# Four gate columns of a graph network's GRU: from a Strassen product for two gates and a plain product for two, to one Strassen product of seven 384-column blocks that shares PSUM banks

## The chip, the cores and the metric

The kernel runs on one core of one Trainium2 chip. The metric is the time of one execution in device microseconds (us), as the median of several runs. Beside the timed runs there is one execution under the hardware profiler; every row, share and moment quoted here comes from that one.

## What is computed

64 graphs of 256 nodes with 256 channels go through two layers. Cut to what matters here, the reference says:

```python
# layer 0
x = layernorm(x + (D^-1/2 adj D^-1/2 + alpha I) @ x @ W.T + b)
# layer 1, x_in has 512 channels
x_conv = relu(bn2(conv17(relu(bn1(conv1(x))))) + x)        # along the nodes
x_nmp  = exp(-dist(x)) @ relu(x @ w_msg.T + b_msg)
x_in   = concatenate([x_conv, x_nmp])
gi = x_in @ w_ih.T + b_ih                                  # 3 * 256 columns: r, z, n
gh = x    @ w_hh.T + b_hh                                  # 3 * 256 columns
r = sigmoid(gi_r + gh_r);  z = sigmoid(gi_z + gh_z)
x = layernorm(x + (1 - z) * tanh(gi_n + r * gh_n) + z * x)
```

Per graph the gates are thus a product of a 256 x 768 input (256 channels of x, 512 of x_in) with weights. Columns r and z need all 768 inputs and add up; column n has to keep its part from x (gh_n) apart from its part from x_in (gi_n), since r multiplies only the first. Counted that way there are four gate columns of 256: r, z, gh_n and gi_n.

## The kernel before, in words

Everything is float32. The 64 graphs go in four quarters (q) of 16 (Q). For each quarter, `layer0` and `layer1` run per graph and leave the spectrum of a 17-tap convolution; the convolution itself is done for the quarter at once, as products by frequency (`products`, matmuls at L542, with combinations of the results on VectorE (DVE) at L585 and L586) and an inverse transform made of many small DVE instructions (`real_transform`, `complex_begin`, `complex_end`). Its result goes to DRAM, and the gates (`gru(g)`) read it back graph by graph.

**What `gru(g)` does.** `load_gate(g + 1)` brings x1 of the next graph (`x_g`, L787) and its transposed inputs (`inputs`, 512 KB, L789) from DRAM through SyncE's (SP's) queue; both tiles have two buffers. `load_conv(g + 2)` (L777) brings the convolution's result for the graph after that. `transposed(g + 1)` makes the last two of the six 128-channel blocks of `inputs`: for graphs of the last quarter and the first four of every quarter (`in_blocks`) a DVE block transpose (L812), an addition on GpSimd (POOL, L813), a small one (L814) and two ScalarE (ACT) activations (L816); for all others TensorE (PE) transposes (L822) and two activations (L824). `input_sums(g + 1)` makes four sums S of quarters of the input on POOL (L833 to L838, 128 x 384 elements each).

The gates r and z are one Strassen-Winograd product. The input is cut into four quarters A11, A12, A21, A22 (two node halves c, two channel halves of three 128-channel blocks) and the weights likewise; four weight quarters are replaced by differences T1 to T4. `block(p, j, a, b)` is one block product: three matmuls of 128 x 128 by 128 x 256 (L854) into half a bank. Seven of them go into the half banks of `p15`, `p26`, `p7` and `p34`, and DVE and ACT combine them in `trz` (L867 to L878). gh_n and gi_n are then a plain product for each node half c: two and four matmuls of 256 columns (L891) into the two halves of a bank `p_n`. DVE and ACT finish from L896 on: bias, r times gh_n, tanh (L903), the mix with z and x1 (L914 to L916), the layernorm (DVE statistics L326 to L328, an inverse root by `pow` on POOL at L329, L332, then two activations at L334), and a store of x1 to `out` from ACT's queue (L918). `trz` and `nn` have one buffer each; PSUM has four rotating banks for these products and for the convolution's (`accbank`), and four more for everything else.

**What sets the order of the work.** Each engine has its own in-order queue, filled by a scheduler from the order of the Python generators. `gru` yields four times; drivers interleave its pieces with other generators. By that, a graph's gates stand in one of four surroundings: between the layers of later graphs (`early` and `others`); between the convolution's products (`take(late, ...)` in the loop over `STEPS`); nearly by themselves with the inverse transform's DVE work inserted behind marked instructions (`paced`, `mark`, `RATES`); or quite by themselves, for the last quarter (`run(gates(q, range(Q)))`).

Of the kernel before, what the change touches and what calls it, by code (L numbers as in the profile page):

```python
# [26 lines left out]
def kernel(  # L27
# [128 lines left out]
    wrz = const.tile([P, 7, HALF, D], F32)  # L156
    B11, B21, B22, T1, T2, T3, T4 = range(7)
    wn = const.tile([P, 3 * DCH, D], F32)
# [265 lines left out]
    def x1_transposed(g):  # L424
# [7 lines left out]
        nc.scalar.copy(xn[:, 1], p[:, 1])  # L432

    def layer1(g, place):
# [4 lines left out]
        x1T = xn[:, :DCH]  # L439
# [80 lines left out]
        nc.scalar.copy(xn[:, DCH:], p)  # L520
# [115 lines left out]
    def turned(re, im, angle):  # L636


        t = freq.tile([P, 2, D], F32, name="turn", bufs=3)
        x, y = M[:, re, :], M[:, im, :]  # L640
        real_part(t[:, int(re > im), :], x, y, angle)
        return imaginary_part(t[:, int(re < im), :], x, y, angle), t
# [4 lines left out]
    def real_transform():  # L647
# [17 lines left out]
        for i, x, y in ((1, 9, 13), (2, 10, 14), (3, 15, 11)):  # L665
            angle = math.pi * ORDER[i] / 8
            t = freq.tile([P, 2, D], F32, name="turn", bufs=3)
# [50 lines left out]
    def output(q, n, re, im):  # L718
# [4 lines left out]
        t = freq.tile([P, 2, D], F32, name="turn", bufs=3)  # L723
# [61 lines left out]
    def load_gate(g):  # L785
# [5 lines left out]
        if in_blocks(g):  # L791
            FIRST[g] = gate.tile([1, N], F32, name="x1_first")
# [14 lines left out]
    def transposed(g):  # L807
# [3 lines left out]
        if in_blocks(g):  # L811
            behind(nc.vector.transpose(xcT.rearrange("p k (s r) -> p k s r", r=RB), CONV.pop(g)))  # L812
            nc.gpsimd.tensor_tensor(xcT, xcT, inputs[:, :DCH], op=ALU.add)  # L813
# [16 lines left out]
    def input_sums(g):  # L830
        A11, A12, A21, A22 = halves(GATE[g][1])
        S = SUMS[g] = gate.tile([P, 4, HALF, P], F32, name="sums", bufs=1)
        nc.gpsimd.tensor_tensor(S[:, 0], A21, A22, op=ALU.add)  # L833
        second = nc.gpsimd.tensor_tensor(S[:, 1], S[:, 0], A11, op=ALU.subtract)  # L834

        with tc.issue_after(second.ins):
            nc.gpsimd.tensor_tensor(S[:, 2], A11, A21, op=ALU.subtract)
            nc.gpsimd.tensor_tensor(S[:, 3], A12, S[:, 1], op=ALU.subtract)  # L838

    def gru(g):  # L840
# [5 lines left out]
        trz = gate.tile([P, 4, D], F32, name="trz", bufs=1)  # L846
        nn = gate.tile([P, NCH, D], F32, name="nn", bufs=1)
# [4 lines left out]
        def block(p, j, a, b):  # L852
            for k in range(HALF):
                nc.tensor.matmul(  # L854
                    p[:, j * D : (j + 1) * D], a[:, k], wrz[:, b, k], start=k == 0, stop=k == HALF - 1
                )

        p15, p26 = accbank("p_rz"), accbank("p_rz")
        block(p15, 0, A11, B11)
        block(p26, 0, A12, B21)  # L860
        block(p15, 1, S[:, 0], T1)
        block(p26, 1, S[:, 1], T2)
        yield
        if following:
            sent(g + 1)
        first = gate.tile([P, 2, D], F32, name="first", tag="gn")
        nc.scalar.copy(first, half(p15))  # L867
        mark(nc.vector.tensor_add(trz[:, 0:2], first[:, 0:1].to_broadcast([P, 2, D]), half(p26)), 1)
        p7, p34 = accbank("p_rz"), accbank("p_rz")
        block(p7, 0, S[:, 2], T3)  # L870
        block(p34, 0, S[:, 3], B22)
        block(p34, 1, A22, T4)
        nc.vector.tensor_add(trz[:, 3], trz[:, 1], p7[:, :D])
        mark(nc.vector.tensor_add(trz[:, 1:3], trz[:, 1:4:2], half(p34)), 1)

        nc.scalar.activation(trz[:, 0:4:2], trz[:, 0:4:2], AF.Tanh, scale=0.5)
        nc.vector.tensor_add(trz[:, 1:4:2], trz[:, 1:4:2], first[:, 1:2].to_broadcast([P, 2, D]))
        nc.scalar.activation(trz[:, 1:4:2], trz[:, 1:4:2], AF.Tanh, scale=0.5)  # L878
        if following:
            transposed(g + 1)  # L880
        yield
        for c in range(NCH):
            terms = [(inputs[:, k, c * P : (c + 1) * P], wn[:, k]) for k in range(3 * DCH)]
            if c == 0 and following:
                input_sums(g + 1)
            if c == 1 and g % Q + 2 < Q:
                load_conv(g + 2)
            p = accbank("p_n")
# [297 lines left out]
```

## Time and profile before

| | |
|---|---|
| timed runs | median 2135.34 us of 3 (2130.76 to 2136.28) |
| the profiled execution | 2128.84 us, span from first to last instruction 2127.1 us |
| TensorE clock granted, mean | 0.99 |
| instructions | 29,376 |
| DVE busy, whole span | 1430.8 us (67%) |
| ACT busy | 879.8 us (41%) |
| POOL busy | 691.1 us (32%) |
| HBM traffic | 296 MB, 139 GB/s over the span |

The profile has a page (busy time of each engine, a picture in 40 slices, the chain of work that ended last, the costliest groups of equal instructions) and a trace that can be asked for windows of time, a timeline and waits. "PE" is the matmul side of TensorE and "PEld" its loading of the stationary operand, which overlaps. A float32 matmul stands in the trace as two PE instructions, each with a PEld instruction of its own; so one block product of three matmuls is six rows. Since matmuls are pipelined, a matmul's own duration overlaps the next one's: its price is the distance from start to start. A row of a group reads: source line, engine, operation, output and inputs, shape, number of instructions | busy time in us, mean ns of one | idle time of the engine before them and what ended it. In the timeline a row is: start in us, duration, engine, line, operation, output and inputs, number of instructions, and in brackets how long the engine had idled and what released it.

### The profile page before, as it was taken

Reading aid. Unit: us, or ns where it says so; the run is one execution under the profiler, and the core shown is the slowest. Engines: PE = TensorE matmul, PEld = TensorE weight load, DVE = VectorE, ACT = ScalarE, POOL = GpSimd, SP = SyncE. Lnnn points to the kernel's source line nnn. Section 1 sums busy time; section 2 is a strip of 40 time slices with the busy share of each in tenths; the row PEclk is TensorE's granted clock in tenths of the full one; section 3 lists DMA queues with packets and bytes.
Section 4 is the critical chain, followed back from the end, with each engine's and each line's share of the span. In section 5 each row is a group of like instructions: output and inputs, shape, how many; then the busy total and the mean of one; then the engine's idle time right before and its main releaser. Section 6 shows DMA issues by size and latency. Waiting matters only on the chain. (4 is left out here: it accounts for less than half of the span.)

```text
span 2127.1 us, 29376 instructions
## 1 busy us (share of the span) xinstructions
PE 2036.4 (96%) x9693; PEld 1736.0 (82%) x9693; DVE 1430.8 (67%) x3467; ACT 879.8 (41%) x2113; POOL 691.1 (32%) x672
## 2 busy tenths in 40 slices
PE   6999999888999999999999999999999999999998
PEld 5888788766888888787888888877888888888887
DVE  5555567775558687774545978775454889976665
ACT  4666643456431234455553123445554122233332
POOL 3445310121431243213321224323331124455553
PEclk9999999999999999999999999999999999999999
DMA  4766656444447644333335754434333745443331
GB/s 125 236 200 196 199 188 210 148 134 123 106 132 219 193 126 133 100 117 101 115 99 157 225 156 132 119 102 132 94 94 99 244 148 141 117 119 95 95 90 50
DMA packets 302918, 298.26 MB, mean 140 GB/s; under 512 B 84112, under 2 KB 281572, under 8 KB 302766
## 3 DMA queue, kind: packets, MB, share of 16 engines
q1 hardware_dynamic: 242814, 200.37, 31.8%
q10 hardware_dynamic: 44480, 67.39, 8.9%
q0 software_dynamic: 15472, 28.61, 6.1%
q8 instruction: 78, 1.28, 0.2%
q14 instruction: 74, 0.61, 0.1%
HBM read 193.19 MB, written 103.06 MB: 139 GB/s over the span
## 5 line engine op out<-in xcount | busy, mean ns | idle before, releaser
L854 PE MATMUL p_rz<-wrz,sums 128*128 128x256 f32 x1536 | 350.9, 381 | 4.7 <-DVE gn L897 4.7
L891 PE MATMUL p_n<-wn,inputs 128*128 128x256 f32 x1536 | 349.2, 380 | 0.0
L854 PEld LDWEIGHTS p_rz<-wrz,sums 128*128 128x128 f32 x1536 | 289.8, 190 | 49.4 <-issue 10.9
L891 PEld LDWEIGHTS p_n<-wn,inputs 128*128 128x128 f32 x1536 | 287.0, 190 | 43.3 <-issue 6.6
L854 PE MATMUL p_rz<-wrz,inputs 128*128 128x256 f32 x1152 | 270.4, 379 | 0.0
L854 PEld LDWEIGHTS p_rz<-wrz,inputs 128*128 128x128 f32 x1152 | 217.9, 190 | 29.2
L370 POOL TENSOR_TENSOR dis<-deg,neg_half 128x2 f32<-128x2 f32 x64 | 46.5, 726 | 540.9 <-DVE deg L368 539.7
L329 POOL TENSOR_TENSOR ln_rs<-ln_rs,neg_half 128x2 f32<-128x2 f32 x129 | 98.8, 766 | 377.8 <-DVE ln_rs L328 349.3
L542 PE MATMUL p_k<-u,VM 128*128 128x256 f32 x736 | 175.1, 381 | 3.9 <-DMA u<-ud 3.0
L903 ACT ACTIVATE nn<-gn 128x256 f32<-128x256 f32 x128 | 53.4, 417 | 270.6 <-DVE gn L900 270.6
L833 POOL TENSOR_TENSOR sums<-inputs 128x384 f32<-128x384 f32 x64 | 66.0, 1031 | 292.2 <-ACT inputs L824 232.7
L542 PEld LDWEIGHTS p_k<-u,VM 128*128 128x128 f32 x736 | 139.0, 190 | 24.2 <-DMA u<-ud 3.2
L447 PE MATMUL p_conv<-wc,xn 128*128 128x259 f32 x512 | 131.6, 397 | 26.6 <-DVE xn L431 25.3
L400 PE MATMUL p_hT<-adjT,x 128*128 128x256 f32 x512 | 125.7, 387 | 15.8 <-DVE adjT L382 13.6
L447 PEld LDWEIGHTS p_conv<-wc,xn 128*128 128x128 f32 x512 | 97.2, 196 | 49.1 <-DVE xn L431 32.5
L509 DVE TENSOR_TENSOR aT<-aT,adjT 128x512 f32<-128x512 f32 x64 | 44.5, 696 | 122.0 <-ACT aT L508 122.0
L410 PE MATMUL p_out<-w,hT 128*128 128x256 f32 x512 | 123.1, 383 | 1.3 <-ACT hT L405 0.7
L483 PE MATMUL p_dft<-fwd,h 128*128 128x240 f32 x512 | 116.8, 371 | 6.4 <-ACT scols L451 6.4
L468 PE MATMUL p_msg<-wmsg,xn 128*128 128x256 f32 x512 | 121.3, 380 | 0.5 <-ACT inputs L824 0.5
L516 PE MATMUL p_nmp<-aT,msg 128*128 128x256 f32 x512 | 121.1, 379 | 0.2 <-DVE aT L509 0.2
L334 ACT ACTIVATE x_g<-x_g,ln_mr,ln_rs 128x256 f32<-128x256 f32 x128 | 70.0, 593 | 123.3 <-DVE ln_mr L332 123.3
L400 PEld LDWEIGHTS p_hT<-adjT,x 128*128 128x128 f32 x512 | 92.8, 192 | 31.8 <-ACT dist_l L498 6.2
(164 smaller groups left out, 3822.1 us busy)
## 6 DMA issues: line engine op xcount, KB each, us to landing
u<-ud SPq DMA_DIRECT2D x284, 256.0 KB
xn_d<-xn ACTq DMA_DIRECT2D x64, 512.0 KB
inputs<-xn_d SPq DMA_DIRECT2D x64, 512.0 KB
ud<-u_set POOLq DMA_DIRECT2D x39, 480.0 KB, 6.0
adj_t<-in_adj_dram SPq DMA_DIRECT2D x64, 256.0 KB
x_t<-in_x_dram SPq DMA_DIRECT2D x64, 256.0 KB
x_d<-x ACTq DMA_DIRECT2D x64, 256.0 KB
xc_d<-VM SPq DMA_DIRECT2D x64, 256.0 KB
```

The lines of the kernel that those rows point to most:

```text
L329: nc.gpsimd.tensor_tensor(rs[:, : len(chunks)], rs[:, : len(chunks)], neg_half[:, : len(chunks)], op=ALU.pow)
L334: nc.scalar.activation(y[:, c, :], y[:, c, :], AF.Identity, bias=mr[:, c : c + 1], scale=rs[:, c : c + 1])
L400: nc.tensor.matmul(p[:, k, :], x1[:, mc, k * P : (k + 1) * P], adjT[:, mc, 1 - mc : 3 - mc, :].rearrange("p n q -> p (n q)"), start=mc == ...
L410: nc.tensor.matmul(p[:, c, :], hT[:, k, c * P : (c + 1) * P], w0[:, k, :], start=k == 0, stop=k == DCH - 1)
L447: nc.tensor.matmul(p, x1T[:, k, c * P : (c + 1) * P], wc1[:, k, :], start=k == 0, stop=k == DCH - 1)
L468: nc.tensor.matmul(p[:, c, :], x1T[:, k, c * P : (c + 1) * P], wmsg[:, k, :], start=k == 0, stop=k == DCH - 1)
L483: nc.tensor.matmul(p[:, t0 * FL : t1 * FL], h[:, c, k * P : (k + 1) * P], fwd[:, first : first + t1 - t0, :].rearrange("p t f -> p (t f)") ...
L516: nc.tensor.matmul(p[:, k, :], msg[:, mc, k * P : (k + 1) * P], aT[:, mc].rearrange("p n q -> p (n q)"), start=mc == 0, stop=mc == NCH - 1,)
L542: nc.tensor.matmul(p[:, j * D : (j + 1) * D], v[:, k, :], u[:, k, :], start=k == 0, stop=k == DCH - 1)
L833: nc.gpsimd.tensor_tensor(S[:, 0], A21, A22, op=ALU.add)
L854: nc.tensor.matmul(p[:, j * D : (j + 1) * D], a[:, k], wrz[:, b, k], start=k == 0, stop=k == HALF - 1)
L891: nc.tensor.matmul(p[:, o * D : (o + 1) * D], lhsT, w, start=j == 0, stop=j == len(part) - 1)
```

## The change

The four gate columns become one Strassen-Winograd product. Each weight quarter now holds, for half of the 256 outputs (HD = 128), three groups of 128 columns for each 128-channel block: [gh_n, r, z] for a block of x, [r, z, gi_n] for a block of x_in. A bank holds the four groups in the order gh_n, r, z, gi_n, so the block of x writes columns 0 to 383 and the two blocks of x_in columns 128 to 511. For this the blocks of `inputs` are put in another order (x, x_nmp, x_nmp, x, then x_conv), so that each channel half begins with one block of x. Seven block products of three matmuls with 384 columns replace seven block products with 256 columns and the twelve plain matmuls.

Three of the seven products are not given a bank of their own: they are added onto a bank that ACT or DVE has read before, with one other product in between. The results are put together in one tile `G` (one buffer), by quarters (c, h): node half c and output half h. Nonlinear work is done on both node halves at once at the end.

The pieces of `gru` are now two, each of two sub-pieces: it yields SOFT inside a piece and HARD at its end, and in the loop over `STEPS` a new driver, `take_whole`, takes whole pieces (where a step took 0, 1 or 2 of the old four). The other changes follow from these: `sums` becomes four tiles with one buffer each, filled in the order 0, 1, 2 and later 3; `x1_first` has one buffer instead of two, `turn` two instead of three; the weights are loaded and prepared in the new layout (16 transfers instead of 11).

The diff, cut to its core:

```diff
-    wrz = const.tile([P, 7, HALF, D], F32)
+    HD = D // 2
+    GN, GR, GZ, GI = range(4)
+    wall = const.tile([P, 7, HALF, 3, HD], F32)
-    wn = const.tile([P, 3 * DCH, D], F32)
...
-        nc.scalar.copy(xn[:, DCH:], p)
+        nc.scalar.copy(xn[:, 1 : 1 + DCH], p)
...
-            FIRST[g] = gate.tile([1, N], F32, name="x1_first")
+            FIRST[g] = gate.tile([1, N], F32, name="x1_first", bufs=1)
...
     def gru(g):
...
-        trz = gate.tile([P, 4, D], F32, name="trz", bufs=1)
-        nn = gate.tile([P, NCH, D], F32, name="nn", bufs=1)
+        G = gate.tile([P, NCH, 2, 4, HD], F32, name="G", bufs=1)
...
+        def product(a, b, p=None):
+            first = p is None
+            if first:
+                p = accbank("p_g")
             for k in range(HALF):
                 nc.tensor.matmul(
-                    p[:, j * D : (j + 1) * D], a[:, k], wrz[:, b, k], start=k == 0, stop=k == HALF - 1
+                    p[:, : 3 * HD] if k == 0 else p[:, HD:], a[:, k], wall[:, b, k].rearrange("p t d -> p (t d)"),
+                    start=first and k == 0, stop=True, skip_group_check=not first or k > 0,
                 )
+            return p
...
+        p1 = product(A11, B11)
+        first = gate.tile([P, 4 * HD], F32, name="first", bufs=1)
+        nc.scalar.copy(first, p1)
+        p6 = product(S[1], T2)
+        mark(nc.vector.tensor_add(quarter(0, 1), first, p6), 1)
+        yield SOFT
         if following:
             sent(g + 1)
+        product(A12, B21, p1)
+        nc.scalar.copy(quarter(0, 0), p1)
+        yield HARD
         if following:
             transposed(g + 1)
+        p7 = product(S[2], T3)
+        nc.vector.tensor_add(quarter(1, 1), quarter(0, 1), p7)
+        p5 = product(S[0], T1)
+        mark(nc.vector.tensor_add(quarter(1, 1), quarter(1, 1), p5), 1)
+        yield SOFT
+        if following:
+            input_sums(g + 1, (0, 1, 2))
+        product(A22, T4, p7)
+        mark(nc.vector.tensor_add(quarter(1, 0), quarter(0, 1), p7), 1)
+        product(S[3], B22, p5)
+        if following:
+            input_sums(g + 1, (3,))
+        if g % Q + 2 < Q:
+            load_conv(g + 2)
+
+        def squashed(c):
+            rz = G[:, c, :, GR : GZ + 1, :].rearrange("p h t d -> p h (t d)")
+            nc.scalar.activation(rz, rz, AF.Tanh, scale=0.5)
+
+        squashed(1)
+
+        def finished(part):
...
+            nc.vector.scalar_tensor_tensor(n, r, 1.0, n, op0=ALU.add, op1=ALU.mult)
...
+            nc.vector.tensor_tensor(i4, i4, bias, op=ALU.add)
+            nc.vector.scalar_tensor_tensor(i, n, 0.5, i, op0=ALU.mult, op1=ALU.add)
+            nc.scalar.activation(i, i, AF.Tanh)
...
+            mark(nc.vector.scalar_tensor_tensor(yq, z, 3.0, yq, op0=ALU.add, op1=ALU.mult), 1)
+            nc.vector.scalar_tensor_tensor(i, z, 1.0, i, op0=ALU.subtract, op1=ALU.mult)
+            nc.vector.tensor_sub(yq, yq, i)
             run(layernorm(y, 4 * LN_EPS))
             nc.scalar.dma_start(out[g].rearrange("(c p) d -> p c d", p=P)[:, part], y)
+
+        if g == B - 1:
+            finished(slice(1, 2))
+        mark(nc.vector.tensor_add(quarter(0, 1), quarter(0, 1), p5), 1)
+        squashed(0)
+        finished(slice(0, 1 if g == B - 1 else NCH))
+        yield HARD
...
+    def take_whole(stage, n):
+
+        for _ in range(n):
+            while next(stage, HARD) != HARD:
+                yield
+            yield
...
-                run(take(late, (0, 1, 1, 1, 1, 1, 2, 1, 2, 1, 2, 1)[step] if more else step % 2))
+                run(take_whole(late, step in ((2, 4, 6, 8, 9, 10, 11) if more else (3, 7, 11))))
```

## The prediction, made before the changed kernel was run

> **What bounds the kernel now.** The page's busy times come first: PE is busy nearly always, DVE two thirds. Then the windows, because such shares mix stages. Then the waits, and last the timeline of the last quarter.
>
> ```profile
> PE 2036.4 (96%) x9693; PEld 1736.0 (82%) x9693; DVE 1430.8 (67%) x3467; ACT 879.8 (41%) x2113; POOL 691.1 (32%) x672
> ...
> L854 PE MATMUL p_rz<-wrz,sums 128*128 128x256 f32 x1536 | 350.9, 381 | 4.7 <-DVE gn L897 4.7
> L891 PE MATMUL p_n<-wn,inputs 128*128 128x256 f32 x1536 | 349.2, 380 | 0.0
> ```
>
> ```profile
> 660.00:735.00 75.00, 75.00 (x353) 66.05 (x352) 62.66 (x124) 14.01 (x28) 17.37 (x16) 1.00 0.73 217
> 1780.00:1866.00 86.00, 81.97 (x385) 70.24 (x383) 81.25 (x177) 23.82 (x50) 39.06 (x34) 1.00 0.48 135
> 1889.00:2117.00 228.00, 228.00 (x1058) 200.61 (x1056) 146.32 (x325) 73.06 (x144) 115.17 (x109) 1.00 0.34 88
> ```
>
> The columns are window, its length, then busy time of PE, PEld, DVE, ACT and POOL (with instruction counts), clock, DMA share, GB/s. Gates waited only 4.7 us in the whole execution. Among the products (first window) and in the last quarter (third) PE never stops; in the second, where the inverse transform runs beside the gates, DVE is busy 94% and PE already loses 4 us.
>
> ```profile
> 2017.39 2.75 PE L854 MATMUL p_rz<-wrz,inputs 128*128 128x256 f32 x12
> 2019.98 5.34 PE L854 MATMUL p_rz<-wrz,sums 128*128 128x256 f32 x24
> 2025.16 1.46 PE L854 MATMUL p_rz<-wrz,inputs 128*128 128x256 f32 x6
> 2026.45 5.34 PE L891 MATMUL p_n<-wn,inputs 128*128 128x256 f32 x24
> 2031.63 2.75 PE L854 MATMUL p_rz<-wrz,inputs 128*128 128x256 f32 x12
> ```
>
> One graph of the last quarter is the distance between equal lines: 2031.63 - 2017.39 = 14.24 us, for 66 PE instructions, so 215.8 ns for 256 columns.
>
> **The matmuls.** The change leaves 7 x 3 x 2 = 42 instructions of 384 columns. None exists in the trace. Nearest rows, start to start: eight dft instructions of 240 columns from 1601.06 to 1602.68 (202.5 ns each), and four 128-column transposes from 1731.07 to 1731.51 (110 ns). Both give 0.83 ns per column with almost no fixed part, so 384 columns cost 215.8 + 128 x 0.83 = 322 ns (ends: 313 from 1.5 x 208, 331 from 1.5 x 221). A graph takes 42 x 0.322 = 13.54 us, 0.70 less; over 64 graphs -44.6 us if PE bounds everywhere. One block product is 1.94 us: that is the time in which ACT or DVE must read a bank before PE wants to add to it.
>
> The weight loads fall from 66 to 42 per graph, yet each (190 ns) lies inside the 215.8 ns from matmul to matmul, so I book nothing for them. The Trainium skill ("Perfetto Trace Analysis", Identifying the Most-Contended Engine) judges TensorE by the busy share of its weight loads and not by that of matmuls; by that rule the 24 loads x 190 ns x 64 = 292 us would be an estimate of the gain, which start-to-start distances of this trace contradict.
>
> **What the 0.70 us must be taken from.** The question in each stage is whether anything else needs more than 13.54 us per graph. Three new ties arise. Three banks are re-used one product later. `G` has one buffer, so the addition of p6 for graph r+1 stands behind the last read of G in graph r's finishing. And two node halves are finished together, so the last tanh (L911) of r sits later, on ACT behind the relus of inputs(r+2).
>
> *Last quarter, 16 graphs.* In the instruction order of the changed kernel ACT has: two tanhs of r, relu of inputs(r+2), the copy `first` of r+1, the other relu, the last tanh of r, the copy of quarter (0,0), layernorm of r, store of r. SP has the load of x_g(r+1), which waits for the store of r-1 (same buffer), then inputs(r+2). So the last tanh of r waits for a transfer that stands on SP behind one which waits for the store of r-1: a loop of one period. Before shows each link:
>
> ```profile
> 2031.83 0.34 SPq L789 DMA_DIRECT2D inputs<-xn_d  x1
> ...
> 2033.55 0.42 ACT L903 ACTIVATE nn<-gn 128x256 f32<-128x256 f32 x1 [2.46 <-DVE gn L900]
> ...
> 2035.61 1.27 POOL L813 TENSOR_TENSOR inputs<-inputs 128x512 f32<-128x512 f32 x1 [5.26 <-DMA inputs<-xn_d]
> ...
> 2036.91 0.51 ACT L816 ACTIVATE inputs<-inputs,bn_bias 128x256 f32<-128x256 f32 x1 [2.95 <-POOL inputs L813]
> ...
> 2037.33 0.56 ACT L867 COPY first<-p_rz 128x512 f32<-128x512 f32 x1
> ...
> 2037.79 0.51 ACT L816 ACTIVATE inputs<-inputs,bn_less 128x256 f32<-128x256 f32 x1
> ...
> 2039.68 0.38 ACTq L918 DMA_DIRECT2D out_dram<-x_g  x1
> ...
> 2041.91 0.36 SPq L787 DMA_DIRECT2D x_g<-x_d  x1
> ```
>
> Tanh end to store: 2039.68 - 2033.97 = 5.71. Store to x_g issue: 2.23. That issue: 0.36. Inputs issue to POOL's addition: 3.78 here, 3.62 to 4.62 over ten graphs, mean 4.0. Addition to relu: 1.30. Relu, copy, relu: 1.39. Tanh of 512 elements (L876): 0.63. Sum 15.62 us against 14.24: +1.38 for some 13.5 graphs = +18.6, less 1.7 for the 2.5 without such a load: **+17**. Ends: with 4.62 for the landing 16.24, +27. If x_g is not in front, inputs(r+2) starts at the end of p7's second use, and 4.0 + 1.30 + 1.39 + 0.63, then on DVE the mix (2 x 0.69), the statistics (1.4) and the additions of p6 and p7 (2 x 0.69), together 4.2, and 1.94 of PE make 13.5, hidden under PE: -9.
>
> *Inverse transform beside gates, 10.5 graphs.* Periods were 15.3 us; DVE at 94% did 14.5 us in each. DVE per graph: before 7.7 us for 14 instructions (0.69 for 512 elements, 0.41 for 256, statistics 1.5); after, 11 of 512 elements and the same statistics, 7.9 to 8.6, I take +0.5, so 15.0 per period. Of these only the addition for quarter (1,0) and some 2 us of inserted work can lie beside the two re-added products; the other 12.3 stand between the end of p5's second use and the start of p7's in the next graph. With 0.2 for the semaphores and 2 x 1.94 of PE the period is 16.4: +1.1 for 8 graphs, -0.7 for two: **+7** (2 if the transform's work fits beside more, 13 if less).
>
> *Merge stretches, 10 graphs* (730 to 830, 1258 to 1340): periods of 15.1 to 16.6 before; the same chain gives 15.2 to 16.3: **0** (-5 to +5).
>
> *Among layers and products, 27.5 graphs.* PE's other work covers the gates' waits, so 27.5 x -0.70 = -19.2 is at hand. But DVE is 84% busy in the first window, with instructions of 0.5 us mean, and the additions of p7 and p5 must pass within 1.94 us; a quarter of the gain goes (-14.5), and some 3 us of new short waits come: **-11.5** (-19 to -4).
>
> *Ends.* The last graph's finishing after the last product has one addition and wider instructions more, +1.2; 16 weight transfers in place of 11 and differences of 1152 elements in place of 768, +0.8: **+2** (1 to 3). ACT gets 0.4 us more per graph, at 41% busy; POOL the same four sums. Both are hidden, except where ACT's order is in the loop above.
>
> **Sum:** 17 + 7 + 0 - 11.5 + 2 = +14.5. Against the profiled execution's 2128.84 us that is 2143.3; the median of the runs is 6.5 above it, so the forecast is **2149.8 us**. Ends of all terms together: -30 and +44, 2105 and 2179. A difference under 0.3% (6.4 us, so 2128.9 to 2141.7) is about what a measurement of this kernel cannot tell from no change.
>
> A sentence of the Trainium skill speaks against this change: "Perfetto Trace Analysis", Optimizing Tensor Performance, says that independent matmul groups should rotate through different banks so that the reading of one overlaps the next one's matmuls. Before had six uses over four rotating banks and 4.7 us of waits in all; here reuse is one product away, and by that rule the 27.5 covered graphs too would gain nothing, a sum of +26.
>
> **Rivals.**
> 1. *PE stays the bound everywhere*: -44.6 + 2 = -42.6, 2093 us. This is the other side. It takes one thing, that the last quarter's loop closes within 13.54 us: the transfer would have to land within 1.9 us in place of 4.0, or SP's x_g not hold up inputs; and that DVE's 12.3 us spread over the period in the transform. For it: 228.00 of 228.00 on PE, with DVE at 64%. Against: the rows of the loop. Chance 0.13.
> 2. *Loops half hidden*: ACT's wait decides, but x_g is out of the way (buffer free early), so the last quarter gives -9 to 0 and the rest goes as forecast, -11.5 to -2.5 in all: 2124 to 2133, down to 2105 with the low ends of the other terms. Chance 0.17.
> 3. *Transfers crowd*: x_g (256 KB) and inputs (512 KB) now start together; by bytes the landing is 4.0 x 1.5 = 6 us, the loop 17.6, the last quarter +27 more, and the product stretches give nothing: 14.5 + 27 + 11.5 = +53, 2188. Chance 0.12.
> 4. *It does not do what it says*: 384 columns at 339 ns or more would take the whole saving; the three rows of 128, 240 and 256 columns leave no room for it. Inside the other chances.
>
> The forecast, 2135 to 2178, has 0.58. Faster: all of rival 1 and two thirds of 2, 0.25. Same: the rest of 2 and the lowest tenth of the forecast, 0.12. Slower: 0.63. The range 2094 to 2180 leaves out rival 3 and the low half of rival 1.
>
> **What would show it.** Right: in the last quarter a `p_g` period near 15.6, PE idle before the second product of p1 or p7, released by ACT or DVE; the last tanh starting right after the second relu; SP's x_g behind the store and inputs behind x_g. With the transform, periods near 16.4. Wrong: periods of 13.5 (rival 1), 384-column starts more than 331 ns apart, or the largest loss among the products.

## The result: 2.5% slower, and the profile after

The changed kernel takes 2184.81 us (median of 4 runs, 2180.82 to 2188.96), the kernel before 2133.05 us in the same set of runs. The ratio is 1.0247, with a 95% interval of 1.0211 to 1.0283. The forecast was 2149.8 us: the direction was right, the loss more than three times as large (about +52 us in place of +14.5), outside the range.

The page of the changed kernel, busy times and the groups of the products:

```profile
PE 2012.9 (92%) x8157; PEld 1438.8 (66%) x8157; DVE 1481.7 (68%) x3348; ACT 906.7 (42%) x2114; POOL 664.6 (30%) x672
...
L859 PE MATMUL p_g<-wall,sums 128*128 128x384 f32 x1536 | 532.6, 489 | 9.0 <-DVE G L884 7.3
L859 PE MATMUL p_g<-wall,inputs 128*128 128x384 f32 x1152 | 417.1, 498 | 62.9 <-ACT first L870 34.1
```

PE has less to do (2012.9 us for 2036.4) and waits more: 72 us at the gates' products, where it was 4.7. The windows, with the columns as before (the last one lies in the last quarter, which now runs from about 1900 to 2165 us):

```profile
660.00:735.00 75.00, 73.27 (x289) 53.11 (x288) 64.29 (x114) 15.98 (x29) 19.04 (x17) 1.00 0.70 203
...
1780.00:1866.00 86.00, 73.96 (x233) 42.35 (x232) 81.19 (x159) 25.07 (x47) 31.25 (x30) 0.98 0.44 116
```

```profile
1915.00:2105.00 190.00, 161.82 (x475) 90.13 (x476) 112.86 (x202) 54.88 (x102) 75.60 (x79) 0.98 0.31 78
```

Among the products PE is still nearly full. Beside the inverse transform DVE is as busy as before (94%) while PE has fallen from 95% to 86%, and in the last quarter PE fell from 100% to 85% with no other engine near its limit (DVE is next, at 59%): the mark of a chain or a loop.

**Where the time went.** Both traces were divided at the same events: first and last matmul of the convolution's products and of the dft, and the stores of `out`. In us, for the profiled executions:

| stretch | before | after | difference | forecast |
|---|---|---|---|---|
| convolution's products (3) | 305.5 | 294.0 | -11.5 | -9.5 for this row and the next: |
| layers, set-up, early gates, end | 1310.4 | 1305.9 | -4.5 | -11.5 covered, +2 at the ends |
| merge stretches (2) | 156.0 | 167.5 | +11.5 | 0 |
| transform beside gates | 159.6 | 177.8 | +18.2 | +7 |
| 14 graphs of the last quarter | 195.5 | 234.7 | +39.2 | +17 |
| all | 2127.0 | 2179.9 | +52.9 | +14.5 |

The stretches come from one profiled execution of each kernel. In the runs below that edit the last quarter alone, the products move between 293.7 and 297.2 us, the merges between 167.4 and 168.4, the transform between 177.8 and 182.0 and the rest between 1301.1 and 1312.4; smaller differences show nothing by themselves.

The gain that the change is made for did arrive where other work covers the gates: -16.0 us with the ends, where 19.2 were at hand without them (the -11.5 of the products are clear of that spread, the -4.5 are not). All of the loss lies in three places where the gates stand nearly by themselves.

### The profile page after: what moved, and what is told of

Its sections match the earlier page's. It is cut to its first block, busy times and chain, and to the rows that moved or that the text cites. A ratio compares the mean times of both kernels' runs of the same rounds, so it can differ in the third digit from the quotient of the medians.

```text
span 2179.9 us, 26251 instructions
## 1 busy us (share of the span) xinstructions
PE 2012.9 (92%) x8157; PEld 1438.8 (66%) x8157; DVE 1481.7 (68%) x3348; ACT 906.7 (42%) x2114; POOL 664.6 (30%) x672
## 4 chain that ended last, share of the span: by engine, by line
PE 52%; DVE 20%; issue 9%; DMA 7%; POOL 5%; ACT 5%; SPq 1%; ACTq 0%; POOLq 0%; DVEq 0%
PE p_g L859 19%; PE p_k L543 7%; PE p_hT L401 4%; PE p_out L411 4%; PE p_conv L448 3%; DMA inputs<-xn_d 3%; PE p_dft L484 3%; PE p_msg L469 3%; PE p_nmp L517 3%; PE p_u L309 2%; POOL ln_rs L330 2%; DVE ln_st L327 2%; DMA out_dram<-x_g 2%; DVE ln_mr L333 2%; PE p_dist L508 2%
## 5 line engine op out<-in xcount | busy, mean ns | idle before, releaser
L859 PE MATMUL p_g<-wall,sums 128*128 128x384 f32 x1536 | 532.6, 489 | 9.0 <-DVE G L884 7.3
L859 PE MATMUL p_g<-wall,inputs 128*128 128x384 f32 x1152 | 417.1, 498 | 62.9 <-ACT first L870 34.1
L859 PEld LDWEIGHTS p_g<-wall,sums 128*128 128x128 f32 x1536 | 289.3, 191 | 204.2 <-issue 11.3
L859 PEld LDWEIGHTS p_g<-wall,inputs 128*128 128x128 f32 x1152 | 212.4, 191 | 224.7 <-DVE G L882 47.8
L839 POOL TENSOR_TENSOR sums<-inputs 128x384 f32<-128x384 f32 x128 | 143.7, 1124 | 274.7 <-PE p_g L859 269.2
L898 ACT ACTIVATE G<-G 128x512 f32<-128x512 f32 x128 | 80.8, 631 | 277.1 <-DVE G L889 198.2
L333 DVE SCALAR_TENSOR_TENSOR ln_mr<-ln_mv,ln_rs 128x2 f32<-128x2 f32 x129 | 53.3, 415 | 100.2 <-POOL ln_rs L330 99.9
L484 PEld LDWEIGHTS p_dft<-fwd,h 128*128 128x128 f32 x512 | 97.8, 192 | 24.1 <-ACT scols L452 15.6
L411 PEld LDWEIGHTS p_out<-w,hT 128*128 128x128 f32 x512 | 95.4, 190 | 27.3 <-ACT hT L406 6.7
```

What stands on the lines that cost most here:

```text
L333: nc.vector.scalar_tensor_tensor(mr[:, : len(chunks)], mv[:, : len(chunks), 0], -1.0, rs[:, : len(chunks)], op0=ALU.mult, op1=ALU.mult)
L411: nc.tensor.matmul(p[:, c, :], hT[:, k, c * P : (c + 1) * P], w0[:, k, :], start=k == 0, stop=k == DCH - 1)
L484: nc.tensor.matmul(p[:, t0 * FL : t1 * FL], h[:, c, k * P : (k + 1) * P], fwd[:, first : first + t1 - t0, :].rearrange("p t f -> p (t f)") ...
L839: nc.gpsimd.tensor_tensor(S[i], x, y, op=op)
L859: nc.tensor.matmul(p[:, : 3 * HD] if k == 0 else p[:, HD:], a[:, k], wall[:, b, k].rearrange("p t d -> p (t d)"), start=first and k == 0, ...
L898: nc.scalar.activation(rz, rz, AF.Tanh, scale=0.5)
```

## The experiments

The theories were: the **loop theory** of the prediction (in the last quarter the last tanh waits behind a transfer), the **bank theory** (adding onto a bank one product after it was used makes PE wait), and, formed from the trace of the changed kernel, the **contention theory** (DVE instructions stand still beside POOL's additions, and the change put DVE onto the path). What gave rise to the third is a pair of rows. Before, the small DVE instruction behind `pow` (`pow` is POOL's line 329) took 0.16 us, since POOL's next addition came later:

```profile
2038.36 0.16 DVE L332 SCALAR_TENSOR_TENSOR ln_mr<-ln_mv,ln_rs 128x2 f32<-128x2 f32 x1 [1.46 <-POOL ln_rs L329]
...
2039.71 0.99 POOL L833 TENSOR_TENSOR sums<-inputs 128x384 f32<-128x384 f32 x1 [1.38 <-ACT x_g L334]
```

After, POOL goes from `pow` straight on to a sum, and the same instruction (now line 333) takes 0.95 us and ends when the sum ends (2066.29 and 2066.28):

```profile
2065.27 1.01 POOL L839 TENSOR_TENSOR sums<-inputs 128x384 f32<-128x384 f32 x1
```

```profile
2065.34 0.95 DVE L333 SCALAR_TENSOR_TENSOR ln_mr<-ln_mv,ln_rs 128x2 f32<-128x2 f32 x1 [0.82 <-POOL ln_rs L330]
2066.22 0.67 DVE L882 TENSOR_TENSOR G<-G,p_g 128x512 f32<-128x512 f32 x1
```

The table gives every run: medians of the timed runs, the ratio to the kernel before on the same chip with its interval, and the stretches of its profiled execution. The runs were made on several chips, so the ratios compare them more closely than the medians do. "Products" are the three stretches of the convolution's, "rest" everything not named.

| run | median | ratio | products | merges | transform | last 14 | rest |
|---|---|---|---|---|---|---|---|
| before | 2133.05 | 1 | 305.5 | 156.0 | 159.6 | 195.5 | 1310.4 |
| changed | 2184.81 | 1.0247 (1.0211 to 1.0283) | 294.0 | 167.5 | 177.8 | 234.7 | 1305.9 |
| e1_tanh_first | 2157.30 | 1.0130 (1.0104 to 1.0157) | 294.6 | 167.4 | 182.0 | 208.9 | 1301.1 |
| e2_three_x | 2183.69 | 1.0257 (1.0228 to 1.0286) | 293.7 | 168.2 | 178.6 | 234.7 | 1305.5 |
| e3_own_bank | 2198.47 | 1.0318 (1.0286 to 1.0351) | 297.2 | 168.2 | 179.1 | 241.1 | 1312.4 |
| e4_no_sums | 2120.11 | 0.9959 (0.9945 to 0.9972) | 285.1 | 156.8 | 153.8 | 226.8 | 1292.3 |
| e5_before_no_sums | 2108.91 | 0.9919 (0.9905 to 0.9934) | 301.6 | 156.0 | 150.2 | 199.0 | 1300.0 |
| e6_tanh_first_no_sums | 2087.67 | 0.9818 (0.9803 to 0.9833) | 285.3 | 156.8 | 153.9 | 196.7 | 1292.1 |
| e7_dve_sums | 2148.37 | 1.0095 (1.0079 to 1.0112) | 293.9 | 168.4 | 178.7 | 201.2 | 1306.2 |
| e8_two_G | 2147.92 | 1.0098 (1.0080 to 1.0116) | 291.4 | 166.8 | 178.2 | 202.9 | 1301.1 |
| e9_mr_on_pool | 2167.91 | 1.0192 (1.0178 to 1.0206) | 307.5 | 163.7 | 165.6 | 230.4 | 1301.5 |
| e10_three_edits | 2136.54 | 1.0041 (1.0028 to 1.0055) | 306.7 | 165.9 | 164.9 | 190.1 | 1304.0 |
| e11_and_dve_sums | 2138.10 | 1.0049 (1.0035 to 1.0063) | 308.7 | 165.5 | 165.6 | 190.2 | 1306.6 |
| e12_before_mr | 2126.76 | 0.9992 (0.9983 to 1.0002) | 302.6 | 156.0 | 158.3 | 195.7 | 1312.2 |
| e13_mr_not_in_products | 2126.45 | 0.9997 (0.9983 to 1.0011) | 295.0 | 168.6 | 165.0 | 189.8 | 1304.4 |
| e14_bias_on_pe | 2139.88 | 1.0055 (1.0037 to 1.0072) | 295.1 | 171.7 | 167.1 | 189.9 | 1318.1 |
| e15_writes_only | 2119.52 | 0.9956 (0.9943 to 0.9969) | 284.7 | 156.8 | 154.1 | 228.4 | 1294.1 |

### e1: the last tanh ahead of the relus

```diff
-            for k in (1, 0):
-                nc.scalar.activation(xcT[:, k], xcT[:, k], AF.Relu, ...)
+            with tc.issue_after(TANH[-1]) if g >= B - Q + 2 else ExitStack():
+                for k in (1, 0):
+                    nc.scalar.activation(xcT[:, k], xcT[:, k], AF.Relu, ...)
```

> One edit, last quarter only: the two relus of inputs(r+2) are put behind the last tanh of r on ACT. Nothing else moves. Loop theory (the period of the last quarter is a loop: last tanh, mix and layernorm, store, x_g on SP, inputs on SP, POOL's addition, relu, last tanh): the tanh no longer waits for a transfer, the loop is cut, and what is left is the arithmetic from the end of p5's second use to the next one. By rows of the changed kernel: 2070.92 to 2074.59 for the additions, tanh and mix up to the last tanh, 0.7 for it, 5.62 from its end to the second use of p7, 3.88 for the two re-added products: 13.9 us per graph in place of 17.0, so 13.5 x -3.1 = -41 us, about 2143 us. Bank theory (the waits come from re-using a bank one product later): the copy of p1 and the addition before p7 stand where they stood, period 16 to 17, 2170 to 2185 us. Transform and merge stretches unchanged under both.

It took some 25 us off (ratio 1.0130 for 1.0247), all of it in the last quarter: 208.9 / 14 = 14.92 us per graph in place of 16.76. A tanh that waits behind the relus, and so behind the transfer, is a cause. ACT's and SP's timelines of the changed kernel show one turn of the loop (the addition of POOL, line 814, started at 2075.28, released by the transfer):

```profile
2060.71 0.62 ACT L911 ACTIVATE G<-G 128x512 f32<-128x512 f32 x1
...
2067.46 0.38 ACTq L918 DMA_DIRECT2D out_dram<-x_g  x1
...
2076.58 0.51 ACT L817 ACTIVATE inputs<-inputs,bn_bias 128x256 f32<-128x256 f32 x1 [4.10 <-POOL inputs L814]
2076.99 0.57 ACT L870 COPY first<-p_g 128x512 f32<-128x512 f32 x1
2077.46 0.51 ACT L817 ACTIVATE inputs<-inputs,bn_less 128x256 f32<-128x256 f32 x1
2077.87 0.62 ACT L911 ACTIVATE G<-G 128x512 f32<-128x512 f32 x1
```

```profile
2069.81 0.37 SPq L788 DMA_DIRECT2D x_g<-x_d  x1
2070.28 0.57 SPq L790 DMA_DIRECT2D inputs<-xn_d  x1
```

Tanh to tanh is 17.16 us, by the links that the prediction named. But 13.9 was expected without the loop and 14.92 came. What lies under it is in e1's own trace: POOL's additions to the inputs now fall onto the mix of the gates.

```profile
2058.64 1.27 POOL L814 TENSOR_TENSOR inputs<-inputs 128x512 f32<-128x512 f32 x1 [2.48 <-DVE G L912]
2059.98 1.05 POOL L815 TENSOR_TENSOR inputs<-inputs,x_first 1x256 f32<-1x256 f32 x1
```

```profile
2059.20 1.25 DVE L917 SCALAR_TENSOR_TENSOR G<-G 128x512 f32<-128x512 f32 x1 [0.70 <-ACT G L913]
2060.49 1.10 DVE L918 TENSOR_TENSOR x_g<-x_g,G 128x512 f32<-128x512 f32 x1
```

Here they take 1.25 and 1.10 us, on the chain. One graph earlier POOL's addition began behind the start of both (at 2045.87), and they took 0.69 us:

```profile
2045.07 0.69 DVE L917 SCALAR_TENSOR_TENSOR G<-G 128x512 f32<-128x512 f32 x1 [0.70 <-ACT G L913]
2045.80 0.69 DVE L918 TENSOR_TENSOR x_g<-x_g,G 128x512 f32<-128x512 f32 x1
```

### e2: three buffers of x_g

```diff
-        x1 = gate.tile([P, NCH, D], F32, name="x1_g")
+        if SPARE:                       # last quarter
+            x1 = spare(g, 0, NCH * D, 3).rearrange("p (c d) -> p c d", c=NCH)
+        else:
+            x1 = gate.tile([P, NCH, D], F32, name="x1_g")
```

> One edit, last quarter only: x_g has three buffers in place of two, so that its load waits for the store of r-2 and not of r-1. The relus still stand before the last tanh. Loop theory: the loop over the store is cut, but a shorter loop stays: inputs(r+2) is issued when p7's second use of r has read the old buffer, lands 3.8 to 5.0 us later, addition 1.3, relus and copy 1.3, last tanh 0.6, then 5.6 to the next second use of p7 and 1.9 for it: 14.8 to 16.0 us per graph, 13.5 x (-2.2 to -1.0) = -30 to -13 us, 2155 to 2172 us. Bank theory: no change, 2185 us.

No change: 234.7 us for 14 graphs as before the edit, and the loop theory's -30 to -13 us did not come. But the run does not test the link through the store, since the edit left it whole. With a third buffer SP's queue holds the load of x_g one graph further ahead, and that load again waits for the store of r-1, with inputs(r+2) behind it as before (lines 927, 797 and 799 are the store and the two loads; the three buffers stand under the name `V`):

```profile
2050.44 0.38 ACTq L927 DMA_DIRECT2D out_dram<-V  x1
```

```profile
2052.70 0.38 SPq L797 DMA_DIRECT2D V<-x_d  x1
2053.97 0.33 SPq L799 DMA_DIRECT2D inputs<-xn_d  x1
```

From store to load it is 2.26 us here, and 2.25 to 2.29 in 12 of the last 13 turns; in the changed kernel it was 2.34 on average. SP's list of waits from 1930 to 2140 us says the same (total, times, longest):

```profile
SPq L797 <- DMA out_dram<-V: 94.9, 13, 9.1
...
SPq L799 <- PE p_g L868: 4.5, 6, 0.8
```

The second line belongs to another loop, from p7's second use over the inputs' transfer, relu, tanh and DVE to p7's second use in the next graph: in six of these turns PE held the inputs up by 0.8 us at most after the store had let x_g go. The periods lie between 15.6 and 17.8 us. What the last quarter would take without the link through the store stays open. The last tanh still starts right behind the second relu:

```profile
2059.93 0.51 ACT L826 ACTIVATE inputs<-inputs,bn_bias 128x256 f32<-128x256 f32 x1 [2.67 <-POOL inputs L823]
2060.34 0.57 ACT L879 COPY first<-p_g 128x512 f32<-128x512 f32 x1
2061.05 0.51 ACT L826 ACTIVATE inputs<-inputs,bn_less 128x256 f32<-128x256 f32 x1
2061.47 0.61 ACT L920 ACTIVATE G<-G 128x512 f32<-128x512 f32 x1
```

So e1 shows that the transfer of the inputs ahead of the tanh is a cause; which of the two links holds the transfer up was not separated.

### e3: a bank of its own in place of adding onto p1

```diff
-        product(A12, B21, p1)
-        nc.scalar.copy(quarter(0, 0), p1)
+        if g >= B - Q:
+            p2 = product(A12, B21)
+            nc.vector.tensor_add(quarter(0, 0), first, p2)
+        else:
+            product(A12, B21, p1)
+            nc.scalar.copy(quarter(0, 0), p1)
```

> One edit, last quarter only: A12 x B21 gets a bank of its own and DVE adds it to the copy of p1, in place of adding onto p1's bank and copying by ACT. So PE no longer waits for ACT's copy `first` before this product; the relus still stand before the last tanh. DVE has one instruction of 0.69 us more per graph. Loop theory: PE's wait moves from the copy to the addition before p7, the period stays at 16.3 to 17.3, total within 8 us of the changed kernel, 2177 to 2193 us. Bank theory: the 30 us that PE waited for ACT's copy in the last quarter go, 2150 to 2160 us.

The last quarter grew by 6.4 us. PE waited 30.0 us for ACT's copy `first` there in the changed kernel; that wait is gone, and 41.5 us are waited for DVE's addition before p7, which was 6.8:

```profile
2056.85 4.03 PE L859 MATMUL p_g<-wall,sums 128*128 128x384 f32 x12
2063.47 2.20 PE L859 MATMUL p_g<-wall,inputs 128*128 128x384 f32 x6 [2.59 <-DVE G L886]
```

The bank theory falls for the last quarter: the edit has one DVE instruction of 0.69 us more per graph, some 10 us in all, too little to hide a gain of 30. (e10 below says the same of all three banks.) A wait named in the list of waits was not the cause; it was where the loop met PE. (Of the 18 us between the two profiled executions 6.4 lie in the last quarter; the rest lies in stretches that the edit does not touch.)

### e4, e5, e6: without POOL's sums, after and before

```diff
+        if g % Q:
+            SUMS[g] = KEPT[-1]          # the sums of the quarter's first graph
+            return
```

> Leaves out part of the computation: the sums S are computed only for the first graph of each quarter and those are used for all, so POOL's four additions (about 1.0 to 1.2 us each) are gone for 60 of 64 graphs. All else stays. Contention theory (DVE instructions stand still while POOL adds: the 128x2 instruction behind `pow` took 0.95 us beside a POOL addition and 0.16 us before the change, where none ran): this instruction goes back to about 0.16 us; the last quarter's loop is 0.8 us shorter, 13.5 x -0.8 = -11 us; in the stretches with the transform DVE's instructions shorten by about 1 us per graph, -10 to -20 us for 20 graphs; together 2155 to 2165 us. If the long duration has another cause, the loop and the transform stay as they are, 2180 to 2188 us.

> A control on the kernel before: the same cut as in e4_no_sums (leaves out the sums S except for the first graph of each quarter, so part of the computation is gone). Theory that the changed kernel has put DVE's work onto the path and so pays for POOL's additions, where the kernel before hid them under PE: before gains little, 0 in the last quarter (PE has no gap there), at most 10 x 0.6 us in the stretch with the transform, some us elsewhere: -5 to -20 us, 2108 to 2123 us. If POOL's additions cost the kernel before as much as the changed one (-65 us), contention is no part of the difference: 2060 to 2075 us.

> The edits of e1_tanh_first and e4_no_sums together (leaves out the sums S except for the first graph of each quarter). Theory: the last quarter has two causes one behind the other, a loop through the transfer (17.0 us) and under it the arithmetic chain on DVE with POOL's additions in its way (15.0 us in e1); without both, 13.6 to 14.3 us per graph; e4's 16.4 falls by 2.1 to 2.8 for 13.5 graphs, so 2120 falls by 28 to 38 us, 2082 to 2092 us. If the 15.0 us of e1 were set by something else (bank re-use, G's one buffer), 15 us stay: 2100 to 2105 us.

These three leave out the sums of 60 graphs. That takes 65 us from the changed kernel (61 by the ratios) and 18 us from the kernel before, more than expected in the first case and as expected in the second. Busy times of DVE, first the changed kernel without sums, then the kernel before without sums:

```profile
PE 1997.3 (94%) x8157; PEld 1439.0 (68%) x8157; DVE 1391.6 (66%) x3348; ACT 907.7 (43%) x2114; POOL 414.7 (20%) x432
```

```profile
PE 2032.5 (96%) x9693; PEld 1736.1 (82%) x9693; DVE 1359.6 (65%) x3467; ACT 882.2 (42%) x2113; POOL 411.5 (20%) x432
```

DVE loses 90 us of busy time without the sums in the changed kernel (1481.7 to 1391.6) and 71 us in the kernel before (1430.8 to 1359.6). So DVE stood still beside POOL in both; before, PE hid three quarters of it, after, it lies on the path. The merge stretches show that purely: 156.0 before with sums or without, 167.5 after, 156.8 after without sums. What the sums cost the changed kernel more than the kernel before is, by stretches, 14.6 us in the transform, 11.4 in the last 14 graphs, 10.7 in the merges, 5.0 in the products and 3.2 in the rest. Without them the transform differs by 3.6 us between the two kernels and the merges by 0.8: no more is left there for the other parts of the change (one buffer for `x1_first`, two for `turn`, the new pieces). DVE's plain work differs by 1391.6 - 1359.6 = 32 us, 0.50 us per graph if all of it lies in the gates, and the prediction took +0.5.

With the loop cut as well (e6) the last quarter takes 196.7 / 14 = 14.05 us per graph, and the changed kernel is 1.0% faster than the kernel before without its sums (0.9818 against 0.9919), about 21 us. That is what the change is worth where neither the loop nor POOL's sums stand in the way, half of the 44.6 us that its matmuls save.

### e7, e8: sums on DVE, two buffers of G

```diff
# e7, on top of e1
+            (nc.vector if g >= B - Q + 1 else nc.gpsimd).tensor_tensor(S[i], x, y, op=op)
# e8, on top of e1, from the last quarter's products on
+            G = spare(g, 0, NCH * 2 * 4 * HD, 2).rearrange("p (c h t d) -> p c h t d", c=NCH, h=2, t=4)
```

> The edit of e1_tanh_first, and in the last quarter the four sums S are made by DVE in place of POOL (about 0.53 us each by 0.69 for 512 elements, 2.1 us per graph; DVE was busy 60% there). Contention theory: the DVE instructions that stood still beside POOL's sums (0.8 us on the 128x2 instruction, 0.2 on the bias addition) are short again, but the sums stand in DVE's queue, two of them ahead of work on the path: 13.9 to 15.0 us per graph against 15.0 in e1, total 2142 to 2157 us. If DVE's queue is what counts and not the contention, 15.5 to 17 us per graph, 2164 to 2185 us.

> The edit of e1_tanh_first, and G has two buffers from the last quarter's products on (so for the stretch with the inverse transform and for the last quarter). The addition of p6 for the next graph then stands on DVE one instruction earlier, before the last step of the mix. Theory that G's one buffer ties two graphs: last quarter 15.0 to 14.0 us, transform stretch 16.6 to 16.0, total 2135 to 2148 us. Theory that DVE's order and POOL's additions set the chain: at most the 0.7 us of one instruction, 14.3 to 15.0, total 2147 to 2158 us.

e7 brings the last quarter from 14.92 to 14.37 us per graph though DVE does 2.1 us more work in each: the instruction behind `pow` is back from 0.95 to 0.16 us there and the bias addition from 0.87 to 0.69. e8 brings it to 14.49 and leaves the transform stretch at 178.2. G's one buffer is worth 0.4 us per graph at most, one instruction, and ties nothing in the transform.

### e9, e12: the product behind `pow` on POOL

```diff
-        nc.vector.scalar_tensor_tensor(mr, mv[:, :, 0], -1.0, rs, op0=ALU.mult, op1=ALU.mult)
+        nc.vector.tensor_scalar(mr, mv[:, :, 0], -1.0, None, op0=ALU.mult)
+        nc.gpsimd.tensor_tensor(mr, mr, rs, op=ALU.mult)
```

> One edit to the changed kernel, in the gates' layernorm of all graphs: the product mean x root (128x2) is made by POOL behind its `pow`; DVE only negates the mean beforehand. DVE's queue then no longer holds an instruction that waits for `pow` (0.66 to 0.83 us) and then stands beside POOL's next addition (0.78 to 0.95 us in place of 0.16). Theory that these DVE stalls, ahead of p7's additions, make the transform stretch long: -1.0 to -1.6 us per graph there, -10 to -16 us; the merge stretches -1 to -4 us each; the last quarter stays in its loop through the transfer, 16.4 to 17 us per graph, -0 to -6 us; total 2158 to 2173 us. Theory that the sums' length on POOL or DVE's plain work decides: transform stretch 175 to 181 us as before, total 2178 to 2190 us.

> A control on the kernel before: the product mean x root made by POOL behind `pow`, as in e9_mr_on_pool. PE has no gap in the last quarter and 0.4 to 0.6 us per graph in the transform stretch, where DVE's instruction waited 0.66 us for `pow`: -0 to -7 us, 2120 to 2130 us. If it falls by as much as e9 does from the changed kernel, the edit does not bear on the difference between the two.

The transform stretch fell by 12.2 us, the merges by 3.8 together, the last quarter by 4.3, as expected: a wait of 0.7 us and a standstill of 0.6 us on one small instruction, in DVE's queue ahead of p7's additions, made two thirds of the transform's loss. The kernel before has nothing to gain from the same edit (0.9992, 0.9983 to 1.0002): there the instruction took 0.21 us on average beside the transform (0.79 in the changed kernel), and its wait for `pow` was hidden. Not expected: the convolution's products took 13.5 us more.

### e10, e11, e13, e14: put together

e10 is e9, e1 and e8 together, with one step of the finishing (L914) moved behind the one that feeds the last tanh; e11 adds e7; e13 is e10 with e9's edit left out among the products; e14 is e13 with the bias of gi_n added by PE:

```diff
# e14
+                nc.tensor.matmul(p[:, GI * HD :], bias_row[:, 0], bias_row[:, i], start=False, stop=True, ...)
...
-            nc.vector.tensor_tensor(i4, i4, bias, op=ALU.add)
```

> A version put together from what was learnt: e9's product on POOL, the last tanh ahead of the relus, two buffers of G from the last quarter's products on, and in the finishing the step that makes y behind the one that feeds the last tanh (0.68 us). The arithmetic chain of the last quarter is 13.9 - 2.0 - 0.7 = 11.2 us, under the 13.54 us of PE, so 13.6 to 14.2 us per graph; the transform stretch as in e9, 162 to 168 us. 2148 - 7 to 12 - 10 to 16 - 2 to 6: 2112 to 2130 us, so from 0.8% faster to no difference from the kernel before. If the contention only moves to other DVE instructions, 2135 to 2148 us.

> As e10_three_edits, and in the last quarter the four sums on DVE (2.1 us per graph). If what is left of the last quarter's excess over 13.54 us is POOL's additions in DVE's way, 13.54 to 13.7 us per graph and 2 to 8 us less than e10; if PE bounds it there already, the same within 3 us; if the sums in DVE's queue delay p7's additions, up to 10 us more.

> As e10_three_edits, but among the convolution's products the product mean x root stays on DVE. In e9 and e10 these three stretches were 4 to 5 us longer than in the changed kernel each, elsewhere the edit saved time. If the edit itself does it there, the three stretches go back (105, 108, 82 us) and the total is 2136 - 10 to 14: 2122 to 2127 us, from 0.3% faster to no difference from the kernel before. If they are longer for another of e10's edits or by chance, 2132 to 2140 us.

> As e13, and for the graphs beside the inverse transform (merge stretches and transform stretch, some 26 graphs) the bias of gi_n is added by two small matmuls per graph (one row of ones, 128 columns; 4 PE instructions, about 0.44 us by 110 ns each) in place of DVE's addition of 512 elements (0.70 us). If DVE's plain work bounds these stretches, 0.7 us less per graph: merges 83 to 80, transform 165 to 158 us, total 10 to 15 us under e13. If the chain over PE bounds them, 0 to 10 us more than e13.

In e10 the last quarter is bound by PE again, 190.1 / 14 = 13.58 us per graph; its window:

```profile
1900.00:2085.00 185.00, 185.00 (x575) 108.98 (x574) 137.22 (x243) 68.86 (x123) 101.02 (x109) 1.00 0.38 100
```

PE never stops here though three banks are used again one product later, so that alone costs nothing. e11 changes nothing there, as it must if PE bounds. e10's total missed its range because of the products again (306.7), and not because the contention moved to other instructions, as the other expectation had it; e13 shows that e9's edit does it there, for they go back to 295.0 without it. Why it does was not settled: in the first of these stretches PE lost 3.8 us (e9) and 4.8 us (e10) in single waits for ACT copies, which points at ACT's order, but no run separates that. e13 is the best version found, at the time of the kernel before: 0.9997 (0.9983 to 1.0011). e14 is slower by 13 us, more than either expectation allowed: the merges and the transform did not shorten when 0.7 us per graph left DVE for PE, so DVE's plain work alone is not their bound in this version. Its rest grew by 14 us, in the set-up and the layers, for a reason that stays open.

### e15: POOL writes and does not read

```diff
-            nc.gpsimd.tensor_tensor(S[i], x, y, op=op)
+            if g % Q:
+                nc.gpsimd.memset(S[i], 0.01)
+                nc.gpsimd.memset(S[i], 0.01)
```

> The changed kernel with POOL's four sums replaced, for all but the first graph of each quarter, by two fills each of the same 128x384 tile (leaves out the sums: S holds a constant). A fill of 128x288 took 0.35 us, so two of 384 some 0.9 us by proportion, about as long as a sum, but POOL reads nothing. If the cost of the sums is that POOL reads SBUF while DVE's two-input instructions want to, it goes as in e4: the 128x2 instruction behind `pow` back to 0.16 us, the transform stretch near 154 us, total 2115 to 2130 us. If it is POOL's occupancy (pow and the additions to inputs late behind the sums), it stays near 2165 to 2185 us.

Each sum but those of a quarter's first graph is left out, and two fills of the same tile stand in its place. They kept POOL as occupied as expected, 0.9 us for each pair:

```profile
L840 POOL MEMSET sums<- 128x384 f32 x240 | 114.8, 478 | 469.6 <-PE p_g L863 469.1
L841 POOL MEMSET sums<- 128x384 f32 x240 | 100.3, 418 | 13.5
```

and yet the time is that of e4 without sums (2119.52 and 2120.11), stretch by stretch, and DVE's busy time is 1390.6 us, as in e4. The instruction behind `pow` over the whole kernel, first in the changed one, then here:

```profile
L333 DVE SCALAR_TENSOR_TENSOR ln_mr<-ln_mv,ln_rs 128x2 f32<-128x2 f32 x129 | 53.3, 415 | 100.2 <-POOL ln_rs L330 99.9
```

```profile
L333 DVE SCALAR_TENSOR_TENSOR ln_mr<-ln_mv,ln_rs 128x2 f32<-128x2 f32 x129 | 31.9, 250 | 100.3 <-POOL ln_rs L330 100.1
```

So it is not POOL's occupancy or a late `pow`. It is POOL's reading of SBUF beside DVE's instructions. The Trainium skill says so ("SBUF — State Buffer", SBUF: two separate sides): DVE and GpSimd share a port pair that is locked for a whole instruction, taken by a DVE instruction with two SBUF inputs only against a GpSimd instruction that reads SBUF. The runs agree: 0.95 us in place of 0.16 beside a sum, nothing lost beside fills, and DVE's additions with one input in PSUM keep their 0.67 to 0.69 us in all 91 cases beside a sum in the changed kernel (L882 and L884).

## Why the prediction was right and wrong, step by step

**Price of the matmuls: right.** 322 ns were extrapolated. In the last quarter's timeline six instructions start 1.93 to 1.94 us apart, 322 ns each, and the undisturbed period is 13.58 us (e10; forecast 13.54, where 42 x 0.322 is 13.52).

**Last quarter: the loop right, its size wrong.** The loop was foreseen; the changed kernel's trace shows it link by link, and e1 shows that the tanh behind the transfer is a cause. Whether the link through the store is needed stays open (e2). The links were too cheap: over 13 turns inputs to addition took 4.68 us (forecast 4.0; x_g's 256 KB go out just ahead, which may be why), tanh to store 6.0 (5.71, the instruction behind `pow` standing beside a sum), store to x_g 2.34 (2.23), x_g to inputs 0.59 (0.36); together 16.87 us, forecast 15.62. With 4.62 for the landing the prediction had 16.24 and +27; less the same 1.7 that is +25. The second miss stands only in the low end and in rival 2, the work thought to lie under the loop: "hidden under PE: -9". The chain without the loop is 14.92 us (e1), of which POOL's sums make 0.87 (14.05 in e6).

**Transform and merges: the failed step.** It reads: "POOL the same four sums. Both are hidden, except where ACT's order is in the loop above." The prediction set the cost of the sums at nothing. They are the same, but in the kernel before their cost fell on DVE instructions with time to spare, and the change put DVE's additions between two uses of a bank and finished two node halves in one chain. Standstills of DVE then reach PE. The term missing from the sum is what e4 and e5 measure: 65 - 18 = 47 us (44 by the ratios), most of the difference between the two kernels, 11.4 us of it in the last quarter. Without the sums the changed kernel is 8 us (profiled) to 11 us (medians) slower than the kernel before, close to the forecast's +14.5, but that is in part luck: the last 14 graphs lose 27.8 us there (forecast 17), and products and rest gain 24.2 (9.5). DVE's extra plain work, +0.50 us per graph, was right. The prediction took DVE's durations from rows as if they belonged to the instruction; the trace of before held the warning: L900 took 0.77 us on average beside the transform and 0.42 in the last quarter, L914 1.16 and 0.68.

**Covered graphs and ends: within the range.** -16.0 us together against -9.5 forecast; most of the 19.2 at hand came. The last stretch from the 61st store to the end took 45.0 us in both kernels where 1.2 more were booked.

**Rivals.** Rival 1 (PE bounds everywhere) is excluded: even without loop and sums the gain is about 21 us and not 42.6. Rival 3 named a time close to the measured one (2188 us) by another way: the landing did not go to 6 us, and the product stretches kept their gain. The warning drawn from the Trainium skill's rule on rotating banks ("Perfetto Trace Analysis", Optimizing Tensor Performance; +26 us) did not come true either: the covered graphs gained, e3 shows no gain from a bank of its own for one of the three, and in e10's last quarter PE never waits.

## What to carry to other kernels

When a change takes slack from an engine that bounds, list what the slack was hiding, contention included: durations read from a trace in which another engine hides them are prices under cover, and whoever moves such an instruction onto the path must ask what runs beside it. Put nothing that waits for a transfer ahead of a step of the running iteration on an in-order queue. And test a wait by taking it away: PE's largest wait here (30 us for a copy) was a meeting point, and removing it moved it.

## What the runs showed of the hardware that was not expected

A 128x2 DVE instruction with two inputs in SBUF takes 0.16 us alone and 0.95 us where it begins just behind the start of a POOL addition of 128x384 that reads SBUF; DVE then ends with POOL, and the trace shows the standstill as busy time, not as a wait. Over the kernel the sums cost DVE 71 us of busy time before and 90 us after. POOL waits as well: in e2's trace its addition to the inputs took 1.70 us in place of 1.26 where it began beside a DVE instruction. Fills by POOL of the same tiles (0.42 to 0.48 us each, 215 us in all) cost DVE nothing that can be seen, 1390.6 us against 1391.6. Per PE instruction, each further column of a float32 matmul costs 0.83 ns from 128 to 384 columns (110 and 322 ns).
